# Moving the last run's weight load behind a scatter, in a fused cross-attention and mixture-of-experts kernel

## The chip, the cores and the metric

The kernel runs on one core of a Trainium2 chip. The metric is the device time in microseconds (us) of one execution. Five engines of the core appear: TensorE (PE; its weight loads are listed apart as PEld), VectorE (DVE), ScalarE (ACT), GpSimd (POOL) and SyncE (SP). SP does no arithmetic; it issues transfers in the order of its own program. GpSimd issues the indirect transfers (gathers and scatters by a list of rows). All transfers are carried out by 16 DMA engines.

## The reference

The input is 32 sequences of 128 tokens with 256 features, and a context of 32 x 128 x 192. There are two residual layers: cross-attention with 16 heads, and a feed-forward layer with 8 experts, of which each token uses the best two. The change touches only the end of the second layer:

```python
logits = einsum('btd,de->bte', x, Wg) + bg            # x is the normalised input
top2_vals, top2_idx = top_k(logits, 2)
scores = softmax(top2_vals)
combine = einsum('btk,btke->bte', scores, one_hot(top2_idx, 8))
h = gelu(einsum('btd,edh->bteh', x, W1) + b1)         # 8 experts, 256 -> 1024
y = einsum('bteh,ehd->bted', h, W2) + b2              # 1024 -> 256
out = einsum('bted,bte->btd', y, combine)
return layer_norm(x + out, gamma, beta)               # then the residual is added
```

## The kernel before, in words

**Stages.** The 4096 tokens lie in 8 blocks of 512. Attention and gating go block by block. Each token's row is written to a table `xrows` in device memory and, as a start value, to a table `total`. Each token is also placed in a list of slots for each of its two experts.

**Runs.** The experts' work is cut into runs of 256 or 128 slots of one expert. A run `m` has these parts: `fetch_who` loads the slots' token numbers and scores; `fetch_rows` gathers the tokens' rows; `fetch_weights` loads the expert's weights (w1, biases b, w2: 1024, 132 and 1024 KB) on SP's queue; `turn` transposes the rows; `hidden` multiplies by w1 on TensorE (line 451) and applies gelu on ScalarE (line 454); `outputs` multiplies by w2 (line 470), adds the bias and scales by the score on VectorE (lines 481 and 487), and adds the result to `total` by an indirect scatter-add from GpSimd, one for each 128 tokens (line 493). A scatter-add waits until those of the run before have landed, since two runs can hold the same token; the list `added` holds the scatters of the latest run. The argument `then` of `outputs` is called once the first tile's scatter has been issued.

**Order.** The whole program runs under a manual schedule: each engine, and each queue, executes its instructions in the order in which the Python code emits them. So moving a call moves its instructions on every engine that it uses, and an SP transfer that waits holds up every SP transfer emitted after it.

**The last runs.** The last run is `L`; each run from `L-4` on has two tiles of 128 tokens. In this stretch the end of the layer is computed too. When the scatters of run L-4 have landed, blocks 3 to 7 of `total` are loaded (`load_sums`; blocks 0 to 2 were done earlier). For each block `measure` takes mean and variance on VectorE, `scale` normalises on ScalarE (line 1127), and `put_out` multiplies by gamma, adds the residual (VectorE, lines 1133 and 1139) and stores the block to the output on SP (line 1140). These stored rows lack what the last four runs add, so tokens of these runs are corrected:

- `fetch_own(sums, total, m, added)` gathers the sums of the run's own tokens from `total` (line 1160), once the scatters in `added` have landed. Because run m's own scatter-add writes to `total`, it waits for this gather.
- `rate(m)` takes mean and variance (lines 148 and 149 on VectorE, 1181 on GpSimd). `patch(m)` computes the corrected rows (lines 1190 and 1192), four VectorE instructions.
- `send(m)` scatters them over the output (line 1203), after all stores of blocks 3 to 7 and the send before it have landed.

L's weights go into the buffer that run L-3 used, so they cannot be loaded before `outputs(L-3)` is done with it. L-1's weights are made to wait for the sums of block 7 (the argument `behind`).

Of the kernel before, what the change touches and what calls it, by code (L numbers as in the profile page):

```python
# [25 lines left out]
def kernel(  # L26
# [96 lines left out]
    DATA = mybir.DependencyInfo(mybir.DependencyClass.Sync, mybir.DependencyReason.DATA)  # L123
# [50 lines left out]
    def bank(name):  # L174
        return ps.tile([P, TB, P], F32, name=name, tag="bank")

    def flat(t):
        return t.rearrange("p t s -> p (t s)")
# [149 lines left out]
    def first_runs(result):  # L328

        count = counted((taken_old,))[:, 0, :]  # L330
        nc.vector.tensor_copy(old, how_many(count, starts, ALU.is_gt, "old_now"))
        yield
        whole = how_many(count, by256, ALU.is_ge, "whole")
        begins, ends = spans(whole, NE)
        add = new(NE, "add128")
        nc.vector.scalar_tensor_tensor(add, begins, -256.0, ebase, ALU.mult, ALU.add)
        yield
        table = tp.tile([P, AHEAD, 2], F32, name="table0")
        its = fill(table[:, :, 0], NE, begins, ends, add, 256)
        yield  # L340
        nc.vector.tensor_copy(table[:, :, 1], its)
        used = new(NE, "now")
        nc.vector.tensor_scalar(used, begins, -1.0, float(AHEAD), ALU.mult, ALU.add)
        nc.vector.tensor_scalar_max(used, used, 0.0)
        nc.vector.tensor_tensor(used, used, whole, ALU.min)
        done(table)
        result.append(used)
        yield
# [34 lines left out]
            tc.add_manual_dep(got.ins, placed.pop().ins.name, DATA, reason="all slots are placed")  # L383
        whos[m] = who

    def fetch_weights(m, into=None, behind=None):

        k, i, nt = order[m]
        e = nc.sync.value_load(tables[k][0:1, i, 1:2], min_val=0, max_val=NE - 1)
        if into is not None:  # L390
            w1t, bt, w2t = into
        elif m % 3 == 1:
            w1t = a2.tile([P, KD, HID], F32, name=f"w1_{m}", tag="v")
            w2t = a2.tile([P, NHC, D], F32, name=f"w2_{m}", tag="v")
        else:
            both = a2.tile([P, 2, KD * HID], F32, name=f"w_{m}", tag="oT")
            w1t = both[:, 0, :].rearrange("p (k h) -> p k h", k=KD)
            w2t = both[:, 1, :].rearrange("p (c d) -> p c d", c=NHC)
        got = nc.sync.dma_start(out=w1t, in_=w1[bass.ds(e, 1)].rearrange("o (k p) h -> p (o k) h", p=P))
        if behind is not None:  # L400
            tc.add_manual_dep(got.ins, behind.ins.name, DATA, reason="other transfers first")
        if into is None:
            bt = f3.tile([P, BW], F32, name=f"b_{m}", tag="b")
        nc.sync.dma_start(out=bt, in_=biases[bass.ds(e, 1)].rearrange("o p f -> (o p) f"))
        nc.sync.dma_start(out=w2t, in_=w2[bass.ds(e, 1)].rearrange("o (k p) d -> p (o k) d", p=P))
        weights[m] = w1t, bt, w2t

    def reach(rows, m):

        return rows[: OLD * TOK, :] if m < AHEAD else rows  # L410
# [19 lines left out]
    def turn(m):  # L430

        nt, xg = order[m][2], rows_of.pop(m)
        px = flat(bank("px"))
        for k in range(KD):
            for t in range(nt):
                j = k * nt + t
                nc.tensor.transpose(px[:, ts(j, P)], xg[:, t, ts(k, P)], ident)  # L437
        xT = a2.tile([P, KD, nt * P], F32, name=f"xT{m}", tag="kT")
        nc.vector.tensor_copy(xT.rearrange("p k s -> p (k s)"), px[:, : KD * nt * P])  # L439
        turned[m] = xT  # L440
# [18 lines left out]
    added = []  # L459

    def outputs(m, then=None):


        nt, who, hT = order[m][2], whos.pop(m), hiddens.pop(m)
        mine = []
        w1t, bt, w2t = weights.pop(m)
        for t in range(nt):
            py = flat(bank("py"))
            for c in range(NHC):
                nc.tensor.matmul(  # L470
                    py[:, :D],
                    lhsT=hT[c // (NHC // 2)][:, c % (NHC // 2), ts(t, P)],
                    rhs=w2t[:, c, :],
                    start=(c == 0),
                    stop=(c == NHC - 1),
                )
            if m == MAIN - 2:
                y = kept_rows[:, t, :]
            else:
                y = f3.tile([P, D], F32, name=f"y{m}_{t}", tag="y")  # L480
            nc.vector.tensor_tensor(y, py[:, :D], bt[:, NHC:], ALU.add)  # L481
            if m == MAIN - 1:
                z = own(sums, m)[:, t, :]
                nc.vector.scalar_tensor_tensor(z, y, who[:, t, 1:2].bitcast(F32), z, ALU.mult, ALU.add)  # L484
                then(t)
                continue
            nc.vector.tensor_scalar(y, y, who[:, t, 1:2].bitcast(F32), None, ALU.mult)  # L487
            if m == MAIN - 4:
                z = own(sums, m)[:, t, :]
                nc.vector.tensor_tensor(z, z, y, ALU.add)  # L490
            if t > 0:
                nc.gpsimd.memset(apart, 0.0)  # L492
            add = nc.gpsimd.indirect_dma_start(  # L493
                out=reach(total, m),
                out_offset=bass.IndirectOffsetOnAxis(ap=who[:, t, 0:1], axis=0),
                in_=y,
                in_offset=None,
                compute_op=ALU.add,
            )


            for other in mine:
                tc.declare_no_dep(add.ins, other.ins, reason="tokens of their own")
            for other in added:
                tc.add_manual_dep(add.ins, other.ins.name, DATA, reason="the run before")
            mine.append(add)
            if t == 0 and then is not None:
                then()
        added[:] = mine
# [36 lines left out]
    first, second = slice(0, HALF), slice(HALF, INNER)  # L546
# [412 lines left out]
    first, used = [], []  # L959
    for j in range(NSTEP - 1):  # L960
# [33 lines left out]
        if j == 5 * NQ:  # L994
            first = first_runs(used)
# [93 lines left out]
    def of_block(t, blk):  # L1089
        return t[ts(blk, TB)].rearrange("b s d -> s b d")  # L1090
# [18 lines left out]
    def measure(blk):  # L1109

        scales[blk] = (
            fs.tile([P, TB, 2], F32, name="mv3", tag="mv3"),
            fs.tile([P, TB], F32, name="rstd3", tag="rstd3"),
        )
        mv, rstd = scales[blk]
        for t in range(TB):
            tile_stats(fs, accs[blk], mv, t)
        deviation(fs, mv, rstd)

    def scale(blk):  # L1120

        acc = accs[blk]
        mv, rstd = scales.pop(blk)
        shift = fs.tile([P, TB], F32, name="shift", tag="shift")
        nc.vector.scalar_tensor_tensor(shift, mv[:, :, 0], -1.0, rstd, ALU.mult, ALU.mult)
        for t in range(TB):
            nc.scalar.activation(
                acc[:, t, :], acc[:, t, :], AF.Identity, bias=shift[:, t : t + 1], scale=rstd[:, t : t + 1]
            )

    def by_gamma(rows):
        w = rows.shape[1]
        nc.vector.tensor_tensor(rows, rows, gamma_sb.unsqueeze(1).to_broadcast([P, w, D]), ALU.mult)

    def put_out(blk):

        acc = accs.pop(blk)
        by_gamma(acc)
        nc.vector.tensor_tensor(acc, acc, xres[blk], ALU.add)
        stored[blk] = nc.sync.dma_start(out=of_block(out, blk), in_=acc)  # L1140
# [3 lines left out]
    L = MAIN - 1  # L1144
# [8 lines left out]
    def own(t, m):  # L1153
        return t[:, m - (L - PATCH + 1)]
# [29 lines left out]
    def patch(m, tiles=slice(0, 2)):  # L1184

        z, base = own(sums, m)[:, tiles, :], own(bases, m)[:, tiles, :]
        mv, rstd = parts.pop((m, tiles.start))
        n = z.shape[1]
        for t in range(n):
            nc.vector.scalar_tensor_tensor(z[:, t, :], z[:, t, :], mv[:, t, 0:1], gamma_sb, ALU.subtract, ALU.mult)  # L1190
        for t in range(n):
            nc.vector.scalar_tensor_tensor(
                z[:, t, :], z[:, t, :], rstd[:, t : t + 1], base[:, t, :], ALU.mult, ALU.add
            )
# [22 lines left out]
    for m in range(AHEAD, X):  # L1217
# [13 lines left out]
        if m == X - 2:  # L1231
            other = weights[m]
# [48 lines left out]
    fetch_own(sums, total, L - 3, added)  # L1281
    for blk in range(OLD, NBLK):
        got = load_sums(blk)
    fetch_weights(L - 1, behind=got)
    hidden(L - 3)
    turn(L - 2)
    measure(3)
    measure(4)
    scale(3)
    outputs(L - 3, lambda: measure(5))  # L1290
    fetch_weights(L)
    hidden(L - 2)
    scale(4)
    measure(6)
# [1 line left out]
    measure(7)  # L1296
    scale(6)
    turn(L - 1)
    put_out(3)
    scale(7)  # L1300
    outputs(L - 2, lambda: put_out(4))
    put_out(5)
    rate(L - 3)
    put_out(6)
# [1 line left out]
        fetch_own(sums, total, m, added)  # L1306
    hidden(L - 1)
    turn(L)
    patch(L - 3)
    put_out(7)  # L1310
    outputs(L - 1, lambda: rate(L - 2))
    nc.vector.tensor_tensor(own(sums, L - 1), own(sums, L - 1), kept_rows, ALU.add)  # L1312
    rate(L - 1)
# [59 lines left out]
```

## Time and profile before

| | us |
|---|---|
| median of 3 runs | 1146.69 (1145.51 to 1147.69) |
| the profiled execution | 1144.71 |
| its span, first to last instruction | 1143.0 |
| TensorE busy | 1109.0 |
| VectorE busy | 600.9 |
| ScalarE busy | 460.7 |
| GpSimd busy | 310.2 |

The profile covers one execution. Its times count from the first instruction. A row of a timeline has the start, the duration, the engine, the line of the kernel, the operation, and what it writes and reads; in brackets stand the idle time before it and what ended that. For an indirect transfer, the row on POOL is the time in which GpSimd writes its descriptors; the data land later. SPq rows are the issue of a transfer on SP's queue. A wait is put down to what came last by the profile; where that had long been done, something else, often a transfer, ended it. The granted TensorE clock was 0.989 of full speed on average.

### The profile page before, as it was taken

What the parts mean: (1) busy time and instruction counts of PE and PEld (TensorE: products, weight loads), DVE (VectorE), ACT (ScalarE), POOL (GpSimd) and SP (SyncE); (2) the same over time, 40 slices, a digit from 0 to 9 for tenths busy, and PEclk for the clock granted to TensorE, in tenths of its full rate; (3) what the DMA queues carried; (4) which work ended last, traced back from release to release, by engine and by line L of the source; (5) the groups of instructions that cost most, each with busy time, mean ns of one, the idle gap of its engine ahead of it and who ended that gap; (6) DMA issues with size and microseconds to landing.
All of it is one profiled execution on the core that took longest, in us unless ns stands there. A gap on an engine that the chain in (4) does not pass through costs nothing. (4 is left out here: it accounts for less than half of the span.)

```text
span 1143.0 us, 19137 instructions
## 1 busy us (share of the span) xinstructions
PE 1109.0 (97%) x6805; PEld 858.2 (75%) x6805; DVE 600.9 (53%) x1516; ACT 460.7 (40%) x1608; POOL 310.2 (27%) x377
## 2 busy tenths in 40 slices
PE   7999999999999999999999999999999999999993
PEld 4666767676666667676667889999898898898883
DVE  4876776766867777858548371122211111112793
ACT  2565363543544543635336122333332332331450
POOL 1000003030030030120311555333433333354555
PEclk9999999999999999999989999999999999999997
DMA  9400101110110101001014568999987887987982
GB/s 311 153 1 19 38 1 20 38 20 2 38 20 2 37 1 38 2 1 39 3 30 154 178 178 242 276 292 328 276 269 234 253 250 235 277 264 233 319 276 65
DMA packets 128576, 154.62 MB, mean 135 GB/s; under 512 B 21920, under 2 KB 113248, under 8 KB 128480
## 3 DMA queue, kind: packets, MB, share of 16 engines
q1 hardware_dynamic: 111520, 131.54, 35.2%
q0 software_dynamic: 15968, 20.79, 8.7%
q8 instruction: 55, 0.90, 0.3%
q10 hardware_dynamic: 992, 1.05, 0.3%
q14 instruction: 41, 0.34, 0.1%
HBM read 125.07 MB, written 28.28 MB: 134 GB/s over the span
## 5 line engine op out<-in xcount | busy, mean ns | idle before, releaser
L454 ACT ACTIVATE hT<-ph,b 128x256 f32<-128x256 f32 (+1 forms) x344 | 145.6, 429 | 324.2 <-PE ph L451 296.6
L733 ACT ACTIVATE pr<-pss,nmax 128x128 f32<-128x128 f32 x512 | 179.1, 401 | 226.9 <-DVE nmax L729 226.9
L451 PE MATMUL ph<-xT,w 128*128 128x256 f32 (+1 forms) x1376 | 244.2, 336 | 0.0
L470 PE MATMUL py<-w,hT 128*128 128x256 f32 x1088 | 242.2, 379 | 0.0
L451 PEld LDWEIGHTS ph<-xT,w 128*128 128x128 f32 x1376 | 219.0, 191 | 21.7 <-issue 0.2
L470 PEld LDWEIGHTS py<-w,hT 128*128 128x128 f32 x1088 | 203.4, 190 | 25.9
L493 POOL DMA_INDIRECT total<-y,who x64 | 105.1, 1642 | 213.7 <-DVE y L487 115.6
L733 ACT ACTIVATION_READ_ACCUMULATOR pr<-pss,nmax 128x1 f32 x512 | 123.9, 242 | 0.0
L698 PE MATMUL pq<-xnT,wq_sb 128*128 128x512 f32 x256 | 115.2, 593 | 0.3 <-DVE xnT L621 0.3
L792 PE MATMUL pw<-wo_sb,oT 128*128 128x256 f32 x512 | 113.3, 379 | 0.0
L481 DVE TENSOR_TENSOR y<-py,b 128x256 f32<-128x256 f32 x66 | 28.0, 424 | 154.8 <-PE py L470 149.6
L792 PEld LDWEIGHTS pw<-wo_sb,oT 128*128 128x128 f32 x512 | 96.0, 190 | 12.6 <-issue 0.2
L439 DVE COPY xT<-px 128x512 f32<-128x512 f32 (+1 forms) x43 | 24.9, 578 | 151.7 <-PE px L437 142.0
L155 POOL TENSOR_TENSOR rstd<-ve,mhalf 128x4 f32<-128x4 f32 x24 | 25.5, 1063 | 269.8 <-DVE ve L154 266.9
L698 PEld LDWEIGHTS pq<-xnT,wq_sb 128*128 128x128 f32 x256 | 48.6, 190 | 61.3 <-issue 57.6
L129 POOL DMA_INDIRECT slots<-info,ati x64 | 62.7, 980 | 113.5 <-DVE ati L927 95.4
L747 DVE TENSOR_TENSOR pr<-pr,rden 128x512 f32<-128x512 f32 x128 | 88.6, 692 | 4.4
L729 DVE TENSOR_REDUCE nmax<-pss 128x4 f32<-128x512 f32 x128 | 79.4, 682 | 16.2 <-PE pss L719 16.2
L719 PE MATMUL pss<-kT,qT 64*128 64x128 f32 x1024 | 69.4, 282 | 4.9 <-issue 4.9
L719 PEld LDWEIGHTS pss<-kT,qT 64*128 64x128 f32 x1024 | 62.1, 190 | 12.8 <-issue 12.4
L422 POOL DMA_INDIRECT xg<-xrows,who x64 | 63.4, 991 | 26.7 <-issue 12.8
L757 PEld LDWEIGHTS ptp<-ident,pr 128*128 128x128 f32 x512 | 57.8, 141 | 17.0 <-issue 16.1
(178 smaller groups left out, 1192.8 us busy)
## 6 DMA issues: line engine op xcount, KB each, us to landing
w<-in_L_ffn_W_dram SPq DMA_DIRECT2D x86, 1024.0 KB
b<-biases SPq DMA_DIRECT2D x43, 132.0 KB
xres<-in_x_dram SPq DMA_DIRECT2D x8, 512.0 KB
xrows<-rows SPq DMA_DIRECT2D x8, 512.0 KB
total<-rows SPq DMA_DIRECT2D x8, 512.0 KB
resid<-xres SPq DMA_DIRECT2D x8, 512.0 KB
acc<-total SPq DMA_DIRECT2D x8, 512.0 KB
out_dram<-acc SPq DMA_DIRECT2D x8, 512.0 KB
```

The lines of the kernel that those rows point to most:

```text
L129: s = nc.gpsimd.indirect_dma_start(out=slots, out_offset=bass.IndirectOffsetOnAxis(ap=at, axis=0), in_=info, in_offset=None)
L422: nc.gpsimd.indirect_dma_start(out=xg[:, t, :], out_offset=None, in_=reach(xrows, m), in_offset=bass.IndirectOffsetOnAxis(ap=whos[m][:, t, ...
L451: nc.tensor.matmul(ph[:, : nt * P], lhsT=w1t[:, k, ts(c, P)], rhs=xT[:, k, :], start=(k == 0), stop=(k == KD - 1))
L454: nc.scalar.activation(hT[c // half][:, c % half, :], ph[:, : nt * P], AF.Gelu, bias=bt[:, c : c + 1])
L470: nc.tensor.matmul(py[:, :D], lhsT=hT[c // (NHC // 2)][:, c % (NHC // 2), ts(t, P)], rhs=w2t[:, c, :], start=(c == 0), stop=(c == NHC - 1),)
L493: add = nc.gpsimd.indirect_dma_start(out=reach(total, m), out_offset=bass.IndirectOffsetOnAxis(ap=who[:, t, 0:1], axis=0), in_=y, in_offse ...
L698: nc.tensor.matmul(pq, lhsT=wq_sb[:, k, ts(2 * q + c, P)], rhs=xnTs[blk][:, k, :], start=(k == 0), stop=(k == KD - 1),)
L719: nc.tensor.matmul(pss[2 * c + h][:, t, :], lhsT=qT[ts(h, DH), c, ts(t, S)], rhs=kT[ts(h, DH), c, ts(t, S)], start=True, stop=True,)
L729: nc.vector.tensor_reduce(nmax, pss[h], AX.X, ALU.max, negate=True)
L733: nc.scalar.activation(pr[:, t, :], pss[h][:, t, :], AF.Exp, bias=nmax[:, t : t + 1], accum_out=den[:, t : t + 1],)
L747: nc.vector.tensor_tensor(pr, pr, rden.unsqueeze(2).to_broadcast([P, TB, S]), ALU.mult)
L792: nc.tensor.matmul(pw[:, :D], lhsT=oTs[blk][:, k, ts(t, S)], rhs=wo_sb[:, k, :], start=(k == 0), stop=(k == NHP - 1),)
```

## The change

1. `fetch_weights(L)` moves from right after `outputs(L-3)` to after `outputs(L-2)` and `put_out(4)`, and its first transfer now waits for the two scatters of L-2 (`behind=added`). `behind` becomes a list for this.
2. In `outputs(L-2)` the order on VectorE changes: before, block 3 was put out ahead of the first tile, and block 4 between the tiles. Now the first tile comes first, then `scale(7)`, block 3, the second tile and block 4.
3. `put_out(7)` comes before `patch(L-3)` instead of after it.

On SP the order after it is: stores 3 and 4, L's three weight transfers, stores 5, 6, 7; before it, the weights came first and then the five stores. No instruction is added or removed on any engine.

```diff
-    def fetch_weights(m, into=None, behind=None):
+    def fetch_weights(m, into=None, behind=()):
...
-        if behind is not None:
-            tc.add_manual_dep(got.ins, behind.ins.name, DATA, reason="other transfers first")
+        for other in behind:
+            tc.add_manual_dep(got.ins, other.ins.name, DATA, reason="other transfers first")
...
-    fetch_weights(L - 1, behind=got)
+    fetch_weights(L - 1, behind=[got])
     hidden(L - 3)
     turn(L - 2)
...
     outputs(L - 3, lambda: measure(5))
-    fetch_weights(L)
     hidden(L - 2)
...
     turn(L - 1)
-    put_out(3)
-    scale(7)
-    outputs(L - 2, lambda: put_out(4))
+
+    def third():
+        scale(7)
+        put_out(3)
+
+    outputs(L - 2, third)
+    put_out(4)
+    fetch_weights(L, behind=added)
     put_out(5)
     rate(L - 3)
     put_out(6)
     for m in range(L - 2, L):
         fetch_own(sums, total, m, added)
     hidden(L - 1)
     turn(L)
+    put_out(7)
     patch(L - 3)
-    put_out(7)
     outputs(L - 1, lambda: rate(L - 2))
```

## The prediction

> **What bounds the kernel now.** The page first: it says which engine fills the span.
>
> ```profile
> span 1143.0 us, 19137 instructions
> PE 1109.0 (97%) x6805; PEld 858.2 (75%) x6805; DVE 600.9 (53%) x1516; ACT 460.7 (40%) x1608; POOL 310.2 (27%) x377
> ```
>
> TensorE is the bound of nearly everything, but it is done before the end. So the second view is TensorE's timeline of the last runs. I write L for the last run, L-1 for the one before.
>
> ```profile
> 1097.03 7.07 PE L451 MATMUL ph<-xT,w 128*128 128x256 f32 x32
> ...
> 1111.28 7.07 PE L451 MATMUL ph<-xT,w 128*128 128x256 f32 x32
> 1118.19 7.07 PE L470 MATMUL py<-w,hT 128*128 128x256 f32 x32
> ```
>
> L-1's hidden layer starts at 1097.03, L's at 1111.28 without a gap, and the last matmul ends at 1118.19 + 7.07 = 1125.26. The span ends at 1143.0, 17.7 us later. What fills this is read in the chain that ended last:
>
> ```profile
> 1112.84 3.19 DMA sums<-total,who
> ...
> 1116.87 1.47 POOL total L493
> ...
> 1119.48 1.77 POOL total L493
> ...
> 1125.03 2.76 DMA sums<-total,who
> ...
> 1133.90 2.39 DMA out_dram<-sums,who
> ```
>
> The chain starts with the last gather of the partial sums of L-1 (issued 1112.84, landed 1116.03). L-1's scatter-add may not start before that gather has read its rows. After it come L-1's two scatters, the sends of L-3, L's gathers and then sends, each waiting for its forerunner. The whole tail after 1116.03 hangs on that one landing. GpSimd's timeline shows what is ahead of it:
>
> ```profile
> 1087.04 1.64 POOL L493 DMA_INDIRECT total<-y,who  x1 [1.41 <-DVE bnst L148]
> ...
> 1090.00 1.60 POOL L493 DMA_INDIRECT total<-y,who  x1 [0.23 <-issue]
> ...
> 1099.41 2.36 POOL L493 DMA_INDIRECT total<-y,who  x1 [4.17 <-DVE acc L1133]
> ...
> 1102.08 1.57 POOL L493 DMA_INDIRECT total<-y,who  x1 [0.26 <-issue]
> ...
> 1108.36 1.06 POOL L1160 DMA_INDIRECT sums<-total,who  x1 [1.94 <-DMA total<-y,who]
> 1109.72 1.55 POOL L1160 DMA_INDIRECT sums<-total,who  x1 [0.30 <-issue]
> 1111.58 0.95 POOL L1160 DMA_INDIRECT sums<-total,who  x1 [0.31 <-DMA sums<-total,who]
> 1112.84 0.95 POOL L1160 DMA_INDIRECT sums<-total,who  x1 [0.30 <-issue]
> ```
>
> The first two rows are the scatters of L-3, the next two those of L-2, then come the gathers for L-2 and L-1. The trace's record of DMA completions gives the landings: L-3's at 1094.68 and 1098.58, L-2's at 1106.92 and 1107.56. GpSimd takes the next transfer about 0.8 us after a landing (1107.56 to 1108.36; 1116.03 to 1116.87). By the same gap 1098.58 leads to 1099.41: the first scatter of L-2 was held by the landing of L-3's second scatter, not by the VectorE work that its row names, since its tile was ready at 1097.9.
>
> Last, the load: in stretches of the trace, the 16 DMA engines have a busy share of 1.07 to 1.10 from 1091 to 1107 (277 to 384 GB/s), 0.59 to 1110, 0.39 to 1113. In the busy stretch lie L's weights, issued here:
>
> ```profile
> 1088.54 0.37 SPq L399 DMA_DIRECT2D w<-in_L_ffn_W_dram  x1
> ```
>
> **The change, part by part.**
>
> *Weights taken out of 1088 to 1103.* L's three transfers (1024 + 132 + 1024 KB) leave this stretch. L-3's first scatter had company from L-1's own weights and keeps 1094.68. Its second had its packets from 1095 to 1098, beside L's w1; without that, 128 packets run as L-1's did alone (1.1 to 1.3 us), so it lands near 1096.5, 2.1 sooner. GpSimd can start L-2's first scatter at 1097.3.
>
> *VectorE's order.* The transposed input of L-1 is copied by 1094.65. Before, block 3 came next (L1133 and L1139, 2.4 us), and L-2's first tile at 1097.11. Now the tile (L481, L487: 0.7 us) is done near 1095.4, block 3 runs to 1097.8, the second tile to 1098.6 (before 1101.0), block 4 to 1101.0. TensorE has the tiles at 1093.7 and 1097.2, so VectorE doesn't wait; the sum of its work, without a gap until 1114.6, is the same. `scale(7)`, earlier, fills ScalarE's idle 0.98 us before 1097.23; nobody waits.
>
> *When the scatters of L-2 land.* First at 1097.3; the second 2.7 later as before, 1100.0. Both with stores 3 and 4 (512 KB each) as their only company. A scatter of L-1 alone took 3.65 and 3.98 us from issue to landing. With a store beside it I take 4.2: both have landed at 1104.2 instead of 1107.56, 3.4 sooner. Bounds: 1103.7 (alone) and 1107.5 (the old 5.5 to 7.5 us each).
>
> *The new wait on SP.* SP takes a waiting transfer 0.1 us after its landing (L-1's weights at 1086.21, block 7's sums at 1086.10). L's w1 goes out at 1104.3. L-1's w1, in the same position, landed at 1091.49, 5.28 us from issue, and all three parts 10.35 us from it. So w1 is there at 1109.6 for a matmul at 1111.28, w2 at 1114.7 for 1118.19. Were w1 later than 1111.3, TensorE would slip, but VectorE idles 4.6 us before L's first addition, waiting for L's gather: the end moves only beyond that.
>
> *What is queued behind it on SP.* Stores 5, 6 and 7. Their data are ready at 1103.3, 1107.0 and (block 7 ahead of the correction of L-3, four instructions, 1.6 us) 1110.0 instead of 1111.6. Store 5 now waits until 1106. All of it is 3.7 MB from 1104.3; at 340 to 384 GB/s, plus 0.5 MB of gathers and 1.4 us of start, it is through by 1117 to 1118.4. The only reader is `send(L-3)`, at 1122.18: 3 us of slack. The correction itself, 1.6 us later, is read by the same send. Both are costed at nothing; without that slack, each microsecond of lateness would be one of the end.
>
> *The gathers, now in the company of the weights.* This is where the gain can go. First gather at 1104.2 + 0.8 = 1105.0. The fourth followed 4.48 later. Before, one of the four took 1.55 instead of 0.95 us, the one with block 7's L1133 beside it; now blocks 6 (to 1107.0) and 7 (1107.6 to 1110.0) both lie beside them. The Trainium skill (SBUF — State Buffer, section on the two separate sides) says that GpSimd can't write descriptors while certain VectorE operations hold the shared port, and is blocked until they end. By the rule, strictly, each block would hold the gathers up by as much as 2 us, so the fourth would go out near 1112 and the end would come 1.7 us later than before. The rows are milder: +0.6 in that gather, +0.7 in L-2's first scatter, nothing in its second, also beside such operations. I take 0.6 more: the fourth goes out at 1110.1.
>
> How long does it take to land? Lightly loaded, L-2's and L-1's gathers took 2.9, 3.3, 3.7 and 3.2 us. Beside the loads of the sums, these two
>
> ```profile
> 1075.51 1.02 POOL L1160 DMA_INDIRECT sums<-total,who  x1 [3.34 <-DMA total<-y,who]
> 1076.84 0.98 POOL L1160 DMA_INDIRECT sums<-total,who  x1 [0.31 <-issue]
> ```
>
> landed at 1081.41 and 1082.89: 5.9 and 6.05 us; two gathers of rows beside weights, at 1063.24 and 1064.60, took 5.4 and 5.1. The Trainium skill (DMA: Bandwidth & Descriptors, section on queues, rings and completion order) has each DMA engine take turns between its queue rows packet by packet. By that alone a gather of 128 KB would lose little to the weights, some 3.5 us, and would land at 1113.6. I go by the four rows, whose mean is 5.6: landing at 1115.7, against 1116.03.
>
> **The sum.** 3.4 us gained at the scatters, 0.6 lost in issuing, 2.4 lost in landing (5.6 against 3.19): 0.3 us sooner, rounding included. The tail shifts with it: L-1's tiles wait for this landing in both, and L-1's scatters, from 1116.5, find the queue nearly empty. Span 1142.7, execution 1144.4 against the 1144.71 profiled (1.7 us lie around the span). The profiled execution was 2.0 us below the median of 1146.69, so the shift is put on the median: **1146.4 us**. A change within 0.2% (2.3 us) of this kernel can hardly be told from none.
>
> **Rivals.**
>
> *Faster: the gathers slip through.* If the queues take turns as the rule says, the fourth gather lands near 1112.6 to 1113.6, and the tail moves up by as much as 3.4 us; there L-1's first tile (ready 1112.3) sets a floor. Time: 1143.6. For it: the rule. Against it: no gather beside a full queue in this trace took under 5.1 us. Also, `send(L-3)` would then be at 1119 and come close to store 7.
>
> *Slower: the gathers queue behind the weights as a scatter did.* The second scatter of L-3, behind L-1's weights and beside L's, took 8.58 us. If the fourth gather takes 8.6, it lands at 1118.7, 2.7 later than now: 1149.4. It decides from 8.2 us on (1110.1 + 8.2 = 1118.3). For it: w1 goes out 0.7 us ahead of the gathers, just as it went out 0.8 ahead of L-3's first scatter. Against it: part of those 8.58 us was its forerunner's landing, and all four gathers measured under load took 6.05 or less.
>
> *The scatters don't land sooner.* If L-2's still take until 1107.5, weights and gathers start as late as now but together: fourth at 1112.84 + 0.6, landing 5.6 later, 1119.0: 1149.7. Against it: the 1098.58 landing that gated them goes with L's weights.
>
> *No effect:* TensorE late by under 4 us, or a landing sooner by 0 to 2 us, leaves the time within 2.3 us.
>
> **How the numbers follow.** The likeliest case, gain and loss nearly equal, has 0.62 and its own range, 1144.4 to 1149.0; the case of no effect lies in it. Gathers slip through 0.18: all of it faster. Gathers queue 0.13 and scatters not sooner 0.07: slower, 0.20 together. A median of this kernel moves by some 1 us either way, as the three runs shown (1145.51 to 1147.69). For 8 in 10 I leave out the half of the fast rival that lies below 1143.0 (0.09) and the half of the slow ones above 1149.7 (0.10). Faster 0.18, same 0.62, slower 0.20; range 1143.0 to 1149.7.
>
> **What would show it.** L-2's scatters at about 1097.3 and 1100.0 and its gathers from 1105; L's w1 issued at 1104.3; DMA share low between 1097 and 1104 and full from 1106 to 1117; the gathers' landing 5 to 6 us after issue; no gap on TensorE at L's hidden layer. I am wrong if the gathers land in under 4 or over 8 us, if L's matmuls start later than 1115, or if `send(L-3)` waits for a store.

## The result, and the profile after

The changed kernel is slower by a little: 1148.84 us (median of 19 runs, 1147.22 to 1150.73) against 1146.37 us for the kernel before (19 runs, 1145.05 to 1148.07). The ratio is 1.0021, with a 95% interval of 1.0014 to 1.0028, that is 1.6 to 3.2 us. The prediction had 1146.4 us, no change that can be told, with a range from 1143.0 to 1149.7. The time lies in that range, but the loss is clear of the noise.

The profiled execution of the changed kernel took 1150.37 us, which is above its median. From its page, span and TensorE:

```profile
span 1148.7 us, 19137 instructions
PE 1109.8 (97%) x6805; PEld 858.6 (75%) x6805; DVE 600.9 (52%) x1516; ACT 461.6 (40%) x1608; POOL 310.5 (27%) x377
```

The two spans differ by 5.7 us, more than the medians do. So the first step is to find where the traces part. L-1's weights are issued on SP just ahead of everything that the change moves. In the trace before this issue is at 1086.21, in the trace after at 1090.31: 4.1 us of the 5.7 arose upstream, in work that is the same in both. The medians differ by 2.5 us in all, so most of the 4.1 belongs to these two executions alone. **From here on times are counted from that issue, "from the mark".** The span ends 56.8 us from the mark before, 58.4 after: 1.6 us, at the lower end of what the medians say.

TensorE in the changed kernel, the last runs of its timeline:

```profile
1107.80 7.07 PE L470 MATMUL py<-w,hT 128*128 128x256 f32 x32
1114.70 7.07 PE L451 MATMUL ph<-xT,w 128*128 128x256 f32 x32
1121.61 7.07 PE L470 MATMUL py<-w,hT 128*128 128x256 f32 x32
```

L's hidden layer follows L-1's output without a gap: the late weights, issued at 1108.13, did not make TensorE wait. GpSimd's timeline has the difference:

```profile
1091.14 1.64 POOL L493 DMA_INDIRECT total<-y,who  x1 [1.37 <-DVE bnst L148]
...
1094.10 1.61 POOL L493 DMA_INDIRECT total<-y,who  x1 [0.23 <-DVE bnst L148]
...
1101.92 1.61 POOL L493 DMA_INDIRECT total<-y,who  x1 [2.53 <-DMA total<-y,who]
...
1103.84 1.57 POOL L493 DMA_INDIRECT total<-y,who  x1 [0.26 <-issue]
1108.95 1.63 POOL L1181 TENSOR_TENSOR rstdp<-vep,mhalf 128x2 f32<-128x2 f32 x1 [3.55 <-DVE vep L1180]
1110.77 1.41 POOL L1160 DMA_INDIRECT sums<-total,who  x1 [0.19 <-issue]
1112.49 1.36 POOL L1160 DMA_INDIRECT sums<-total,who  x1 [0.30 <-issue]
1114.15 0.96 POOL L1160 DMA_INDIRECT sums<-total,who  x1 [0.30 <-issue]
1115.41 1.24 POOL L1160 DMA_INDIRECT sums<-total,who  x1 [0.30 <-issue]
```

These are the scatters of L-3 and L-2, then a power (line 1181, the inverse square root of the variance in `rate(L-3)`), then the four gathers. In the trace before, the row of this power was:

```profile
1104.79 1.63 POOL L1181 TENSOR_TENSOR rstdp<-vep,mhalf 128x2 f32<-128x2 f32 x1 [1.15 <-DVE vep L1180]
```

From the mark it ended at 20.2 us before and at 20.3 after; the landing of L-2's scatters moved from behind it to ahead of it. The next table has the landings too, from the trace's record of DMA completions:

| us from the mark | before | predicted | after |
|---|---|---|---|
| second scatter of L-3 landed | 12.4 | 10.3 | 10.8 |
| first, second scatter of L-2 issued | 13.2, 15.9 | 11.1, 13.8 | 11.6, 13.5 |
| L-2's scatters landed | 21.35 | 18.0 | 17.62 |
| first gather issued | 22.15 | 18.8 | 20.46 |
| fourth gather issued | 26.63 | 23.9 | 25.11 |
| it took | 3.19 | 5.6 | 6.12 |
| and landed | 29.82 | 29.5 | 31.23 |
| end of the span | 56.80 | 56.5 | 58.37 |

The scatters landed 3.7 us sooner (predicted: 3.4), and the fourth gather landed 1.4 us later. What comes after that landing takes the same time in both, 27.0 and 27.1 us. The chain that ended last in the changed kernel, as the profile follows it, has the power and the gathers in a row:

```profile
1108.95 1.63 POOL rstdp L1181
1110.58 0.19 issue
1110.77 1.41 POOL sums L1160
1112.18 0.30 issue
1112.49 7.72 DMA sums<-total,who
...
1121.43 0.36 DVE kept_rows L487
1121.80 0.58 issue
1122.38 1.63 POOL total L493
```

It goes over L-2's second gather (7.72 us), since VectorE waits for it in `rate(L-2)` before it handles L-1's second tile. But the scatter at 1122.38 is that of the first tile, which VectorE had ready at 1116.8, and 0.58 us before it are unexplained. It also waits for the fourth gather. This landed at 1121.54, and the scatter left 0.84 us later, just as before (1116.03 and 1116.87). So I take the fourth gather's landing to have released it; the other runs, below, show the same gap.

### The profile page after: what moved, and what is told of

Read it like the earlier page. It is cut to its first block, busy times and chain, and to the rows that moved or that the text cites. A ratio compares the mean times of both kernels' runs of the same rounds, so it can differ in the third digit from the quotient of the medians.

```text
span 1148.7 us, 19137 instructions
## 1 busy us (share of the span) xinstructions
PE 1109.8 (97%) x6805; PEld 858.6 (75%) x6805; DVE 600.9 (52%) x1516; ACT 461.6 (40%) x1608; POOL 310.5 (27%) x377
## 4 chain that ended last, share of the span: by engine, by line
PE 86%; DMA 7%; issue 3%; POOL 2%; DVE 2%; ACT 1%; SPq 0%; POOLq 0%; ACTq 0%; DVEq 0%
PE py L470 16%; PE ph L451 16%; PE pw L792 10%; PE pq L698 10%; PE pss L719 6%; PE po L778 5%; PE pk L663 5%; PE ptp L757 5%; PE pv L687 5%; DMA total<-y,who 3%; PE pv L674 3%; PE pk L657 3%; PE ptx L620 1%; PE px L437 1%; DMA acc<-total 1%
## 5 line engine op out<-in xcount | busy, mean ns | idle before, releaser
L719 PEld LDWEIGHTS pss<-kT,qT 64*128 64x128 f32 x1024 | 62.1, 190 | 12.4 <-issue 12.0
L422 POOL DMA_INDIRECT xg<-xrows,who x64 | 63.5, 993 | 28.0 <-issue 13.2
```

The costliest lines, as they stand in the source:

```text
L422: nc.gpsimd.indirect_dma_start(out=xg[:, t, :], out_offset=None, in_=reach(xrows, m), in_offset=bass.IndirectOffsetOnAxis(ap=whos[m][:, t, ...
L719: nc.tensor.matmul(pss[2 * c + h][:, t, :], lhsT=qT[ts(h, DH), c, ts(t, S)], rhs=kT[ts(h, DH), c, ts(t, S)], start=True, stop=True,)
```

## The experiments

Two causes stand in the trace: the power on GpSimd ahead of the gathers (the queue theory), and the weights beside the gathers (the load theory). A third is the new order on VectorE. The first four expectations use the tail from the last matmul to the end as their measure. That was a poor choice: the work in this tail hangs on a chain of landings, not on TensorE, and TensorE ended 37.5 to 39.3 us from the mark in these traces. I give it, and judge by the time from the mark and by the ratio. The runs were made on chips with different times of the kernel before (1130 or 1145 us); each ratio is against that kernel on the same chip. Times from the mark are of the one profiled execution, and the kernel before has 56.8 us.

**Only the weights moved.** In `outputs(L - 2, ...)` and for block 7 the old order is kept.

```diff
     put_out(3)
     scale(7)
     outputs(L - 2, lambda: put_out(4))
+    fetch_weights(L, behind=added)
```

> Only the weights of L are moved behind the scatters of L-2; VectorE keeps its old order. Measure: the tail from the end of the last matmul to the end of the span, 17.7 us before, 20.0 us after the whole change. Load theory (the loss comes from the gathers running beside the weights): tail 19.3 to 20.5, time ratio to before 1.0015 to 1.003. Order theory (the loss comes from the new order on VectorE): tail 17.2 to 18, ratio 0.9995 to 1.0005.

Measured: ratio 1.0024 (1.0014 to 1.0034), 59.6 us from the mark, tail 20.3. L-2's scatters landed at 19.8, the gathers took 7.0, 7.6, 7.8 and 7.2 us, the fourth landed at 32.6. The loss comes with the move of the weights.

**Only VectorE's order changed.**

```diff
     outputs(L - 3, lambda: measure(5))
+    fetch_weights(L)
     hidden(L - 2)
...
     put_out(4)
-    fetch_weights(L, behind=added)
```

> Only the order on VectorE is changed (L-2's tiles first, block 7 ahead of the correction); the weights of L stay where they were. Load theory: the scatters of L-2 still wait for L-3's landing beside the weights, so the gathers leave 0 to 1 us sooner under the old light load: tail 16.9 to 17.7, ratio 0.999 to 1.000. Order theory: tail 19 to 20, ratio 1.0015 to 1.002.

Measured: ratio 0.9991 (0.9983 to 1.0000), 56.5 us, tail 18.1 (between the two expected ranges). The order is no loss; a gain is not clear of the interval. As expected the first scatter of L-2 was still held: L-3's second scatter landed at 12.0 and it left at 12.9. For the scatters both parts of the change are needed: L-2's landed at 21.0 with the order alone, at 19.8 with the weights alone, at 17.6 with both (before: 21.35).

**The power taken out of the gathers' way.** The whole of `rate(L-3)` moves, so on VectorE block 6 comes ahead of it too.

```diff
-    rate(L - 3)
     put_out(6)
     for m in range(L - 2, L):
         fetch_own(sums, total, m, added)
+    rate(L - 3)
```

> The whole change, with rate(L-3) emitted after the gathers of L-2 and L-1, so that its power on GpSimd, which waits for VectorE, no longer stands ahead of them. Queue theory (that power is the main loss): gathers leave 0.8 us after L-2's scatters have landed, about 2 us sooner than in the changed kernel, and land 2 us sooner: tail 18 to 18.4, ratio 1.0000 to 1.0005. Load theory: the first gathers leave sooner but land behind the weights nearly as late; tail 19.2 to 20, ratio 1.0012 to 1.002.

Measured: ratio 1.0005 (0.9997 to 1.0013), 57.9 us, tail 20.4. The gathers left at 18.6, only 0.8 us after the scatters' landing, and the fourth at 23.8 instead of 25.1. But now they took 6.8, 7.1, 7.4 and 6.8 us, and the fourth landed at 30.5, just 0.7 sooner. The tail is above even the load theory's range, the ratio lies at the edge of the queue theory's. From the mark 0.5 us of the loss is gone; the ratios of this kernel and the changed one (1.0005 and 1.0021) put it at 1.8 us, and their intervals together allow about 0.6 to 3. So the size of this gain is not settled. The four gathers show that part of what the earlier issue wins is waited for behind the weights: the fourth left 1.3 us sooner and landed 0.7 sooner.

**The weights left out.** L computes with the weights of L-1; all else as changed.

```diff
-    fetch_weights(L, behind=added)
+    weights[L] = weights[L - 1]
```

> The whole change, with the three weight transfers of L left out: L computes with the weights of L-1. The order of all else stays, so the power of rate(L-3) still stands ahead of the gathers. Load theory: gathers leave at the same place as in the changed kernel but land in 3.0 to 3.7 us instead of 6.1 to 7.7; tail 16.5 to 17.2, ratio 0.9987 to 0.9995. Queue theory: most of the loss stays; tail 19 to 19.8, ratio 1.001 to 1.002.

Measured: ratio 0.9988 (0.9981 to 0.9995), 55.5 us, tail 16.3. GpSimd's gathers in this kernel:

```profile
1092.77 1.41 POOL L1160 DMA_INDIRECT sums<-total,who  x1 [0.20 <-issue]
1094.48 1.36 POOL L1160 DMA_INDIRECT sums<-total,who  x1 [0.30 <-issue]
1096.15 0.95 POOL L1160 DMA_INDIRECT sums<-total,who  x1 [0.30 <-issue]
1097.41 1.24 POOL L1160 DMA_INDIRECT sums<-total,who  x1 [0.30 <-DMA sums<-total,who]
```

They leave 20.5, 22.2, 23.9 and 25.1 us from the mark, as in the changed kernel, and GpSimd spends the same 1.41, 1.36, 0.95 and 1.24 us in them. So the longer writing is not due to the load; the same VectorE work lies beside it in both. But they take 4.3, 3.3, 3.8 and 3.3 us instead of 7.7, 7.7, 6.5 and 6.1. Besides the weights only store 5 differs, which leaves SP 2.0 us sooner. So this is the cost of the load: 2.9 us from the mark (58.4 to 55.5), 3.8 by the ratios (1.0021 and 0.9988). The time in which the gathers are issued and land shows it in the DMA share too. The rows have a stretch, its length, the busy time and number of instructions of PE, PEld, DVE, ACT and POOL, the granted clock, the DMA share and GB/s. Changed kernel, 17.8 to 31.2 us from the mark:

```profile
1108.10:1115.40 7.30, 7.30 (x36) 6.42 (x35) 7.16 (x13) 0.00 (x0) 5.36 (x4) 1.00 0.89 277
1115.40:1121.50 6.10, 6.10 (x30) 5.32 (x29) 3.12 (x11) 3.32 (x7) 1.24 (x1) 1.00 1.03 350
```

The second row's stretch in the kernel before, and then in the kernel without the weights:

```profile
1111.30:1117.40 6.10, 6.10 (x30) 5.38 (x29) 4.21 (x13) 2.84 (x6) 2.44 (x3) 1.00 0.50 150
1097.30:1103.50 6.20, 6.20 (x31) 5.45 (x30) 5.79 (x19) 2.84 (x6) 3.17 (x4) 1.00 0.40 126
```

The gathers should land in this stretch. The DMA share is 1.03 in the changed kernel, 0.50 before and 0.40 without the weights. VectorE (the third pair) is busy 3.12 us in the changed kernel and 5.79 without the weights: it waits for the gathers.

**Half of the weights.** w1 and the biases as changed, w2 left out: L multiplies by the w2 of L-1.

```diff
-    fetch_weights(L, behind=added)
+    fetch_weights(L, behind=added, half=weights[L - 1][2])
```

> The whole change, with w2 of L left out (L multiplies by the w2 of L-1); w1 and the biases are loaded as in the change. Counted from the issue of L-1's w1, the last thing on SP that the change leaves alone, to the end of the span: 56.8 us before, 58.4 changed, 55.5 with no weights of L. If a gather waits for the bytes that stand in the queue ahead of it, the first gather of L-2 lands 5 to 6 us after its issue instead of 7.7, and the end is at 56.3 to 57.2 us, ratio to before 0.9995 to 1.0005. If the queues take turns and only the presence of a load counts, it lands in 7 to 7.7 us and the end stays at 57.8 to 58.4.

Measured: ratio 1.0005 (0.9997 to 1.0013), 56.9 us. The end lies half way between none (55.5) and all (58.4). The gathers took 6.7, 5.6, 5.3 and 4.7 us: the first 1.0 us less than with all weights, between the two expectations, the fourth 1.5 us less. (Of the first gather only 8 of 16 completions are on record.) In the record of packets, the first rows of the gathers move 3.0 us after the first issue with no weights, 4.9 with half and 5.9 with all: most of the time that the load adds to the first gather lies before its rows move. Two of the runs above add to this. Where only the weights moved, and where the power stood behind the gathers, SP issued w1 and the biases ahead of the first gather and w2 behind it. The first gather took 7.0 and 6.8 us there, about as with half the weights, and the other three 6.8 to 7.8. So the cost grows with the bytes that are under way, and neither of the two pictures in the expectation holds alone.

**The power moved with no weights.** This asks for the queue theory's worth once the load is gone.

```diff
-    fetch_weights(L, behind=added)
+    weights[L] = weights[L - 1]
...
-    rate(L - 3)
     put_out(6)
     for m in range(L - 2, L):
         fetch_own(sums, total, m, added)
+    rate(L - 3)
```

> The whole change without the weight transfers of L (L computes with the weights of L-1), and with rate(L-3) emitted after the gathers. With no weights in the way, the power on GpSimd is the only thing between the landing of L-2's scatters (17.6 us after the issue of L-1's w1) and the gathers: the fourth gather leaves at 22 to 23 us instead of 25.1 and lands at 25.3 to 26.5; the end, 55.5 us without this step, comes to 52.8 to 53.8, ratio to before 0.9965 to 0.9977. If the first tile of L-1 (VectorE) is the floor instead: 54.3 to 55.3.

Measured: ratio 0.9969 (0.9959 to 0.9978), 54.3 us from the mark. The first gather:

```profile
1106.50 1.02 POOL L1160 DMA_INDIRECT sums<-total,who  x1 [3.47 <-DMA total<-y,who]
```

It now waits for the scatters alone. The fourth gather left at 23.5 and landed at 27.3, both about a us later than I expected, because L-2's second scatter took 5.25 us in this execution and landed at 18.7. The ratio is in the expected range; the 54.3 us are not, and lie at the edge of the second case. But VectorE's first tile, that case's cause, was ready at 26.9, and L-1's first scatter left at 28.2, 0.85 us after the fourth gather's landing. Against the run with no weights and the power in place the end is 1.2 us sooner, or 2.2 by the ratios (0.9969 and 0.9988). So the power has a price of its own.

**The weights still later.** They wait for L-2's gathers (`own_got` holds the gathers of each run).

```diff
-    fetch_weights(L, behind=added)
...
-    rate(L - 3)
     put_out(6)
-    for m in range(L - 2, L):
-        fetch_own(sums, total, m, added)
+    fetch_own(sums, total, L - 2, added)
+    fetch_own(sums, total, L - 1, added)
+    fetch_weights(L, behind=own_got[L - 2])
+    rate(L - 3)
```

> The weights of L wait for L-2's two gathers instead of its scatters, and rate(L-3) is emitted after the gathers. L-2's gathers then run without the weights. The fourth gather leaves near 24 us after the issue of L-1's w1; its landing meets w1 and takes 3.5 to 5.5 us. TensorE waits for w1 some 3 to 5 us. If the gathers set the end: 55.0 to 56.5 us, ratio 0.9985 to 0.9998. If TensorE's wait now sets it: 57 to 58.5 us, ratio 1.0002 to 1.0015, and VectorE's wait before L's first addition is no longer for the gather.

Measured: ratio 1.0002 (0.9993 to 1.0010), 56.9 us. The gathers took 2.8, 3.6, 3.2 and 3.2 us and the fourth landed at 25.2, 4.6 us sooner than before. All of that was lost again. TensorE's timeline of this kernel, L's hidden layer:

```profile
1115.91 10.14 PE L451 MATMUL ph<-xT,w 128*128 128x256 f32 x32 [3.80 <-DMA w<-in_L_ffn_W_dram]
```

And GpSimd's, L-1's two scatters and the first send:

```profile
1113.83 1.63 POOL L493 DMA_INDIRECT total<-kept_rows,who  x1 [2.01 <-DVE kept_rows L487]
...
1116.44 1.61 POOL L493 DMA_INDIRECT total<-kept_rows,who  x1 [0.23 <-DVE sums L1318]
...
1123.59 1.06 POOL L1205 DMA_INDIRECT out_dram<-sums,who  x1 [4.56 <-DMA out_dram<-acc]
```

TensorE waits 3.8 us for w1, and L's hidden layer then takes 10.14 us instead of 7.07: the granted clock was 0.50 of full speed from 1116 to 1121. The scatters of L-1, now the ones beside the weights, took 8.3 and 6.7 us instead of 3.7 and 4.0. And the send of L-3 waits 4.56 us for store 7, which stood behind the weights on SP. The last is the wait that my prediction had given 3 us of slack. The span ended 20.6 us after this send, as in the kernel before (20.8), so of the three it is this wait that set the end; the profile's own chain names w1 and TensorE instead.

**The weights split.** w1 and biases in their old place; w2, the part that L needs 7 us later, waits for L-1's gathers and is emitted after store 7. With `later=True`, `fetch_weights` issues w1 and the biases and returns the call that issues w2. `rate(L-3)` stands after the gathers.

```diff
     outputs(L - 3, lambda: measure(5))
+    second = fetch_weights(L, later=True)
...
-    fetch_weights(L, behind=added)
...
     put_out(7)
+    got = second()
+    for other in own_got[L - 1]:
+        tc.add_manual_dep(got.ins, other.ins.name, DATA, reason="gathers first")
```

> VectorE's order as in the change; w1 and the biases of L are issued where they were before, w2 of L waits for the gathers of L-1 and is emitted after store 7; rate(L-3) after the gathers. Load theory: L-2's scatters meet only half of the old load and the gathers none, so the fourth gather leaves 24 to 25 us after the issue of L-1's w1 and lands 3 to 3.7 us later; TensorE has w2 in time or waits under 2 us; end at 54.8 to 55.8 us, ratio 0.9980 to 0.9992. If w1 in its old place costs the scatters as much as all the weights did: end near 56.5, ratio 0.9995 to 1.0002.

Measured: ratio 0.9990 (0.9983 to 0.9997), 55.5 us. L-2's scatters landed at 19.8; the gathers in the timeline

```profile
1106.45 1.02 POOL L1165 DMA_INDIRECT sums<-total,who  x1 [3.06 <-DMA total<-y,who]
...
1111.03 0.95 POOL L1165 DMA_INDIRECT sums<-total,who  x1 [0.30 <-issue]
```

took 3.1 to 3.8 us and the fourth landed at 28.4. TensorE's waits have this line:

```profile
PE py L475 <- DMA w<-in_L_ffn_W_dram: 2.3, 1, 2.3
```

TensorE waits 2.3 us, and L's output then takes 8.83 us instead of 7.07, at a granted clock of 0.69 from 1121 to 1126. The end does not feel it: L's first addition on VectorE is at 40.4 us from the mark, 1.2 us sooner than before.

**The same with the power left ahead of the gathers.**

> As the run before it, but with rate(L-3) left ahead of the gathers. If GpSimd's power in that place costs time once the load is gone: gathers leave 0.5 to 1.5 us later than in the run before it and the end is later by as much, ratio 0.0004 to 0.0012 higher. If not: the same end within 0.3 us.

Measured: ratio 0.9988 (0.9982 to 0.9995), 55.5 us; fourth gather issued at 25.1 in both. Here the power costs nothing: L-2's scatters landed at 19.8, and the power was done at 20.3, nearly together. Both split versions beat both kernels: the one before by 0.10 and 0.12%.

**w1 behind L-3's scatters.**

```diff
-    second = fetch_weights(L, later=True)
+    second = fetch_weights(L, behind=added, later=True)
```

> As the split version with rate(L-3) after the gathers, but w1 and the biases of L wait for L-3's scatters, so that they fall between these and the scatters of L-2; w2 waits for the gathers of L-1. If w1 is then through before L-2's scatters move their rows, these land at 18 to 19 us after the issue of L-1's w1 (19.8 in the split version), the fourth gather leaves at 23 to 24 and lands at 26.5 to 27.5; end 53.9 to 55.0, ratio 0.9975 to 0.9985. If w1 holds up L-2's scatters as much as it held up L-3's: end 55.3 to 56.2, ratio 0.9987 to 0.9995.

Measured: ratio 0.9992 (0.9984 to 1.0000), 55.6 us, both within the second case. L-3's second scatter landed at 10.7, but L-2's two then took 7.9 and 7.0 us beside w1 and landed at 20.5. The weights only change which indirect transfers they delay.

## Why the prediction was wrong

The sum was: 3.4 us gained at the scatters, 0.6 lost in issuing the gathers, 2.4 lost in their landing. Measured, against the kernel before: 3.7 gained, 2.2 lost in issuing (7.49 us from the scatters' landing to the fourth issue, before 5.28), 2.9 lost in landing (6.12 against 3.19). The net is 1.4 us later instead of 0.3 sooner.

- **Right:** the landing of L-3's second scatter held L-2's first. It fell from 12.4 to 10.8 without L's weights beside it, and stayed at 12.0 when the weights stayed. Also right: VectorE's order (L-2's first tile at the predicted place, nobody else late), SP taking w1 0.2 us after the landing, no wait on TensorE, no effect of stores 5 to 7 on the send in the changed kernel.
- **The step that failed** is "First gather at 1104.2 + 0.8 = 1105.0". It takes GpSimd to be free once the scatters have landed. Ahead of the gathers in GpSimd's program stands the power of `rate(L-3)`, and its operand comes from VectorE, in whose program it stands after block 5. In the trace before, this row was there to be read at 1104.79, but it ended 1.1 us before the scatters' landing, so it cost nothing. The change moved the landing ahead of it. It didn't move VectorE's `rate(L-3)`, whose place in the sum of VectorE's work is the same. So the first gather left at 20.5 from the mark and not at the predicted 18.8: of the 3.7 us by which the scatters landed sooner, 2.0 could not be had. My account listed what the change adds to SP's queue, and not what stood in GpSimd's between the two transfers of interest. At the end this step cost 1.2 us in the run with no weights (2.2 by the ratios) and 0.5 us in the changed kernel (1.8 by the ratios). The run with the power behind the gathers is the kernel that I had described: its first and fourth gather left at 18.6 and 23.8 from the mark (predicted: 18.8 and 23.9), and its ratio, 1.0005, can't be told from no change.
- **Mis-sized:** the landing beside the weights, 5.6 us by the mean of four rows. It was 6.1 to 7.7 here, and 6.8 to 7.4 where the gathers left earlier. The four rows had 128 KB transfers beside the blocks' sums or the tail of a weight load; here the weights had been issued within 0.6 to 2.6 us before. The nearer row was the scatter that left 0.8 us after w1 (7.64 us); I used its neighbour only for the slow rival, which named the right mechanism at too high a price (8.6 us).
- The Trainium skill's rule of turns between queues, which I set aside for the rows, would by my estimate have given 3.5 us; 6.1 to 7.7 were measured beside the weights, 3.3 to 4.3 without. By my strict reading of its rule of the shared port, blocks 6 and 7 would have held the gathers up by as much as 2 us each. I misread that rule. By the same section of the Trainium skill (SBUF — State Buffer, the two separate sides) a `tensor_tensor`, as on lines 1133 and 1139, has no two-port mode and contends with GpSimd's reads only. From the first to the fourth issue it was 4.65 us against 4.48 before: three of the four rows are 0.3 to 0.5 us longer than the shortest, as one was before by 0.6, and none by 2. The longest such row in any run, 1.97 us where the power stood behind the gathers, is 1.0 us longer. The 0.6 that I took was 0.2.
- **The main cause**, shown by leaving the weights out: without the load the change would gain (0.9988); with it, it loses (1.0021). The load used to fall on the scatters of L-3 and L-2. Of what they lose by it, the part up to the end of GpSimd's power is not felt. It now falls on the gathers, and the end follows their landing. In all kernels here but the one with the weights still later, L-1's first scatter left 0.84 to 0.86 us after the fourth gather had landed, and the span ended 27.0 to 27.4 us after this landing, wherever it fell: at 32.6 from the mark with only the weights moved, 31.2 in the changed kernel, 29.8 before, 29.5 with only the order changed, 28.5 without the weights, 27.3 without the weights and with the power moved.
- **Neither slower rival came true**, though the time is on their side: the gathers took at most 7.7 us, where the first decides from 8.2 on, and the scatters did land sooner. And none of the three signs that were to show me wrong appeared: no gather under 4 or over 8 us, no late start of L's matmuls, no send that waits for a store. All three watched what the weights would do; none watched what stands in GpSimd's own program.

## What to carry to other kernels

A bulk load that is moved out of the way of one indirect transfer will meet the next one: price it at its new place, by the row that left just behind such a load. When a wait ends sooner, read in that engine's program what stands between it and the step that should profit; work that was hidden behind the wait becomes the bound. A load made of two parts with different due times can be split, so that each part lies where no transfer of the end's chain is under way.

## What the runs showed of the hardware

- The four gathers of L-2 and L-1 (128 KB each, by GpSimd) took 2.8 to 4.3 us with no weight load beside them, 4.7 to 6.7 with 1.2 MB of weights and 6.1 to 7.8 with 2.2 MB issued on SP around them. A scatter-add of 128 KB took 3.8 to 4.0 us at the end of the kernel with no weights beside it, where all its completions are on record, and 5.5 to 8.6 us beside weights. Half the bytes gave half the loss at the end (55.5, 56.9, 58.4 us from the mark). The gathers' first rows moved 5.9 us after the first issue in the changed kernel, 3.0 us without the weights. What in the DMA engines makes them wait was not tried.
- After a landing, SP issued the transfer that waited for it within 0.1 to 0.3 us, GpSimd after 0.8 to 0.9 us. So of two transfers released by one landing, SP's bulk load went first here: w1 0.58 us ahead of the first gather where nothing else held the gather back (18.55 against 17.97 from the mark).
- A wait on TensorE cost more than its length: after one of 3.8 us the granted clock was 0.50 from 1116 to 1121, 0.90 from 1121 to 1126, and 32 matmuls took 10.14 us instead of 7.07. The clock missing in these two windows, half of 5 us and a tenth of 5 us, makes up nearly all of the difference. After a wait of 2.3 us (another kernel) it was 0.69 from 1121 to 1126 and 32 matmuls took 8.83. What sets the clock was not tried.
